# A four-layer graph network in one kernel: keys and queries from one projection, and the first node tile loaded in parts

## The chip, the cores and the metric

The kernel runs on one core of one Trainium2 chip. The metric is device time in microseconds (us) of one execution; lower is better. All executions quoted here were in the fast state, except one single run (named below) whose state is not known, and every kernel gave correct outputs.

## The reference, cut to what matters

There are 3327 nodes with 256 features. Four layers run one after the other, each as `x = layernorm(x + layer(x, adj))`. Layer 1 (graph convolution and a state-space scan) is not touched. The parts that the change touches:

```python
# layer 0
deg = adj.sum(axis=1, keepdims=True) + 1.0
neigh = adj @ features / deg
out0 = jnp.concatenate([features, neigh], axis=-1) @ W.T

# layer 2: attention on the graph; its normalised output is layer 3's X

# layer 3: two steps, each with a fresh attention over all nodes
for n in range(2):
    q = Xa @ W1.T @ W2.T             # 64 columns
    k = Xa @ W3.T                    # 64 columns
    A = top_p(softmax(q @ k.T))      # keeps the largest 90% of each row's mass
    Xf = R @ Xf                      # R: row-normalised adjacency with ones added
    Xa = A @ Xa
    Z = Z + Xf @ U1[n].T + Xa @ U2[n].T
```

## The kernel before

Nodes are cut into 26 tiles of 128. TensorE does nearly all of the arithmetic in float32. A record is one line of the trace; one float32 matmul with a 128-row operand appears there as two, so "four records" below are two instructions.

Layer 0 loads all features at once, then works tile by tile. `aggregate` streams one tile's adjacency column blocks and sums 26 products (the 257th column is ones and gives the degree):

```python
def aggregate(atp, psum, it, rhs, cols, jh=JH):          # JH = 13 blocks a load
    acc = psum.tile([P, cols], F32, name="acc")
    for j0 in range(0, nt, jh):
        m = min(jh, nt - j0)
        at = atp.tile([P, jh, P], F32, name="at")
        nc.sync.dma_start(at[:, :m, :], a["adjT"][it][:, j0:j0 + m, :])
        for j in range(m):
            nc.tensor.matmul(acc, at[:, j, :], rhs[:, j0 + j, :], ...)
    return acc
# ... layer 0:
xa = pool.tile([P, nt, D + 1], F32, name="xa")
nc.sync.dma_start(xa[:, :, :D], a["x"])                  # all features, 3.4 MB
nc.vector.memset(xa[:, :, D:], 1.0)
w0 = load(pool, "w0")
for it in range(nt):
    xt = work.tile([P, D // P, P], F32, name="xt")
    nc.sync.dma_start(xt, a["xT"][:, :, it * P:(it + 1) * P])
    acc = aggregate(atp, psum, it, xa, D + 1)
    # ... divide by the degree, transpose, product with w0, add, layernorm
```

Keys and queries are made tile by tile, at the end of layer 2 for step one and inside step one for step two. The 3328 padded nodes are two halves of 13 tiles. A key of the first half is kept on partitions 0 to 63, one of the second half on partitions 64 to 127, so that both halves use all partitions. A query is needed on both sets of partitions. In the kernel before, the weights are simply doubled (`wk` holds W3 twice, `wq` the query weights twice), and each tile pays two 128-column projections:

```python
def query(work, pq, xt):
    for k in range(2):
        nc.tensor.matmul(pq, wq[:, k, :], xt[:, k, :], start=(k == 0), stop=(k == 1))
    q = work.tile([2 * DA, P], F32, name="q")
    nc.scalar.copy(q, pq)
    return q

def key_and_query(work, ps, p, it, xt):
    for k in range(2):
        nc.tensor.matmul(ps[:, 0, :], wk[:, k, :], xt[:, k, :], start=(k == 0), stop=(k == 1))
    h, j = divmod(it * P, half)
    nc.scalar.copy(kT[p][h * DA:(h + 1) * DA, j:j + P], ps[h * DA:(h + 1) * DA, 0, :])
    nc.sync.dma_start(qd[p][it], query(work, ps[:, 1, :], xt))
```

Half of each key projection is thrown away. Layer 2 calls this one tile late, between two tiles' sums, so that the chain that normalises a tile has time to end:

```python
for it in range(nt):
    # ... VectorE builds the attention weights into "at" (two instructions for 13 blocks), 26 products into acc
    if it:
        project(it - 1)                    # transpose X of the tile before, then key_and_query
    # ... VectorE and ScalarE: divide, elu, add, statistics
    power(rs, mv)                          # GpSimd, two small instructions
    nc.gpsimd.tensor_scalar(X[:, it, :], o, mv[:, 0:1], rs, op0=ALU.subtract, op1=ALU.mult)
project(nt - 1)
```

## Time and profile before

| what | value |
|---|---|
| time, median of three runs (lowest, highest) | 4009.58 us (4000.31, 4012.51) |
| profiled run | 4007.87 us, span 4006.0 |
| matmul records on TensorE | 15071, busy 90% of the span |

The first lines of the page of the kernel before (busy us, share of the span, count of each engine):

```profile
span 4006.0 us, 41676 instructions
...
PE 3596.0 (90%) x15071; PEld 2625.0 (66%) x15071; DVE 2724.7 (68%) x6003; ACT 1675.1 (42%) x2690; POOL 367.1 (9%) x436
```

90% does not say where TensorE is free. The table of stretches of the same kernel does, here cut where the stages hand over to each other: at the last summing record of layer 0, the first of layer 2, the first of layer 3 and the last attention sum of step one (rows: layer 0; layer 1; layer 2; step one of layer 3; the rest. Columns: stretch, length, busy us and count of PE, PEld, DVE, ACT, POOL, granted clock, DMA share, GB/s):

```profile
0.00:362.00 362.00, 345.93 (x1602) 300.00 (x1603) 61.41 (x210) 22.04 (x55) 0.69 (x6) 1.00 0.46 153
362.00:1715.90 1353.90, 1125.40 (x3536) 654.14 (x3534) 1159.51 (x1145) 684.51 (x1230) 98.92 (x92) 0.92 0.11 36
1715.90:2068.80 352.90, 337.47 (x1612) 288.46 (x1613) 237.79 (x284) 43.50 (x130) 57.26 (x80) 0.96 0.37 125
2068.80:3034.40 965.60, 941.37 (x4503) 728.71 (x4504) 415.01 (x1410) 320.89 (x594) 28.39 (x56) 0.99 0.18 54
3034.40:4006.00 971.60, 845.79 (x3822) 653.70 (x3820) 850.96 (x2955) 604.14 (x681) 181.80 (x203) 0.94 0.19 54
```

The reader is to see that layer 0, layer 2 and step one leave TensorE idle for only 16, 15 and 24 us, and that the 16 us of layer 0 are the opening, before the first matmul.

### The profile page before, as it was taken

The page shows a single profiled execution, that of the slowest core. Times are in us where ns is not written, and L with a number is a line of the kernel's source. Part 1 is how long each engine was busy: PE and PEld are TensorE (multiplying, and loading weights), DVE is VectorE, ACT ScalarE, POOL GpSimd, SP SyncE. Part 2 cuts the span into 40 slices and gives each one's busy share as a digit, 9 for nine tenths or more (in the row PEclk, how much of TensorE's full clock was granted, in tenths as well). Part 3 has the DMA queues.
Part 4 walks back from the last instruction along what each step waited for, and adds up shares of the span by engine and source line. Part 5 has one row for each costly group of instructions (what it writes and reads, how often), then busy time and mean ns, then how long its engine had stood idle before and what let it go on. Part 6 is the DMA issues. An engine that isn't in the chain of part 4 may idle for free.

```text
span 4006.0 us, 41676 instructions
## 1 busy us (share of the span) xinstructions
PE 3596.0 (90%) x15071; PEld 2625.0 (66%) x15071; DVE 2724.7 (68%) x6003; ACT 1675.1 (42%) x2690; POOL 367.1 (9%) x436
## 2 busy tenths in 40 slices
PE   8999988888888877689999999999999899999985
PEld 7888754444444433378877777777777677777764
DVE  1111589999999989867743443443452999999996
ACT  0000555455554555211112333333344666666662
POOL 0000000101010101011110000000000122222210
PEclk9999999999999988889999999999999999999997
DMA  6442211111111000044422111121102122122100
GB/s 218 138 143 92 76 50 40 35 40 35 35 35 37 20 0 0 15 146 142 142 83 75 56 59 49 52 60 57 46 24 86 58 62 62 53 61 61 54 22 7
DMA packets 98960, 252.96 MB, mean 63 GB/s; under 512 B 13858, under 2 KB 48034, under 8 KB 98610
## 3 DMA queue, kind: packets, MB, share of 16 engines
q1 hardware_dynamic: 98738, 250.14, 20.0%
q8 instruction: 122, 2.00, 0.2%
q14 instruction: 100, 0.82, 0.1%
HBM read 239.88 MB, written 10.22 MB: 62 GB/s over the span
## 4 chain that ended last, share of the span: by engine, by line
PE 34%; DVE 16%; ACT 3%; issue 2%; POOL 2%; DMA 0%; POOLq 0%; ACTq 0%; DVEq 0%
PE acc L751 11%; PE acc L719 7%; PE acc L649 6%; PE sc L707 3%; DVE cand L759 3%; DVE e L892 2%; DVE e L893 2%; PE tp L747 2%; PE pj L917 1%; DVE z L829 1%; DVE top L768 1%; DVE z L873 1%; DVE rest L770 1%; ACT junk L827 1%; ACT junk L848 1%
## 5 line engine op out<-in xcount | busy, mean ns | idle before, releaser
L403 DVE TENSOR_TENSOR_SCAN h<-dA,carry,db 128x512 f32<-128x512 f32 (+1 forms) x448 | 510.7, 1191 | 0.1
L459 PE MATMUL y<-h,ident 128*128 128x512 f32 (+1 forms) x896 | 436.1, 633 | 76.7 <-DVE h L406 76.6
L759 DVE MAX8 cand<-e 128x8 f32<-128x128 f32 x676 | 143.8, 280 | 494.6 <-ACT e L708 494.6
L751 PE MATMUL acc<-G,wt 128*128 128x256 f32 x1352 | 342.9, 408 | 48.4 <-ACT wt L749 48.4
L459 PEld LDWEIGHTS y<-h,ident 128*128 128x128 f32 x896 | 185.9, 215 | 290.8 <-issue 175.9
L749 ACT COPY wt<-tp 128x512 f32<-128x512 f32 (+1 forms) x364 | 185.9, 552 | 438.3 <-PE tp L747 438.2
L751 PEld LDWEIGHTS acc<-G,wt 128*128 128x128 f32 x1352 | 268.9, 204 | 120.7 <-ACT wt L749 82.2
L234 PE MATMUL cb<-F,at 128*128 128x256 f32 x1352 | 334.2, 393 | 9.3 <-ACT m L251 9.2
L708 ACT COPY e<-sc 128x416 f32<-128x416 f32 (+1 forms) x416 | 192.5, 508 | 327.8 <-PE sc L707 327.8
L751 PE MATMUL acc<-X,wt 128*128 128x256 f32 x1352 | 326.0, 386 | 3.0 <-ACT wt L749 2.8
L719 PE MATMUL acc<-X,at 128*128 128x256 f32 x1352 | 320.8, 387 | 2.7 <-POOL e L701 2.7
L234 PEld LDWEIGHTS cb<-F,at 128*128 128x128 f32 x1352 | 261.1, 196 | 90.9 <-issue 33.5
L649 PE MATMUL acc<-F,at 128*128 128x257 f32 x1352 | 311.2, 384 | 2.5 <-DVE at L646 2.5
L719 PE MATMUL acc<-F,at 128*128 128x256 f32 x1352 | 308.8, 380 | 0.0
L113 PE MATMUL acc<-xa,at 128*128 128x257 f32 x1352 | 308.3, 381 | 0.0
L719 PEld LDWEIGHTS acc<-X,at 128*128 128x128 f32 x1352 | 250.8, 191 | 76.1 <-issue 41.8
L751 PEld LDWEIGHTS acc<-X,wt 128*128 128x128 f32 x1352 | 250.3, 191 | 63.8 <-ACT wt L749 33.5
L388 ACT ACTIVATE dA<-dt,A_log 128x512 f32<-128x512 f32 (+1 forms) x448 | 280.9, 681 | 12.6 <-DVE dt L365 12.2
L707 PE MATMUL sc<-kT,q 64*128 64x416 f32 x832 | 259.8, 561 | 26.0 <-ACT e L708 26.0
L113 PEld LDWEIGHTS acc<-xa,at 128*128 128x128 f32 x1352 | 255.7, 191 | 37.5 <-issue 0.7
L719 PEld LDWEIGHTS acc<-F,at 128*128 128x128 f32 x1352 | 249.5, 189 | 46.5 <-issue 13.7
L649 PEld LDWEIGHTS acc<-F,at 128*128 128x128 f32 x1352 | 254.1, 192 | 37.4 <-DVE at L646 2.7
(297 smaller groups left out, 5358.7 us busy)
## 6 DMA issues: line engine op xcount, KB each, us to landing
at<-in_adjT SPq DMA_DIRECT2D x104, 832.0 KB, 4.4
at<-in_adjT SPq DMA_DIRECT2D x156, 448.0 KB, 3.3
at<-in_adjT SPq DMA_DIRECT2D x52, 576.0 KB, 3.7
at<-in_adjT SPq DMA_DIRECT2D x52, 320.0 KB, 2.9
at<-in_adjT SPq DMA_DIRECT2D x26, 512.0 KB, 3.5
xa<-in_x SPq DMA_DIRECT2D x1, 3328.0 KB, 13.5
xt<-in_xT SPq DMA_DIRECT2D x26, 128.0 KB, 4.0
qd<-q SPq DMA_DIRECT2D x52, 64.0 KB, 1.5
```

Of the source, the lines that this page charges most:

```text
L113: nc.tensor.matmul(acc, at[:, j, :], rhs[:, j0 + j, :], start=(j0 + j == 0), stop=(j0 + j == nt - 1))
L234: nc.tensor.matmul(acc, at[:, j % JC, :], X0[:, j, :], start=(j == 0), stop=(j == nt - 1))
L388: nc.scalar.activation(dA[:, g, :], dt[:, g, :], AF.Exp, scale=A[:, g, s:s + 1])
L403: nc.vector.tensor_tensor_scan(h[:, g, :], dA[:, g, :], db[g // 2][:, g % 2, :], initial=carry[:, s, g:g + 1], op0=ALU.mult, op1=ALU.add)
L459: nc.tensor.matmul(ys[g][:, :w], ident, h[:, g, :], start=False, stop=(s == DS - 1))
L649: nc.tensor.matmul(acc, at[:, j, :], F[:, j0 + j, :], start=(j0 + j == 0), stop=(j0 + j == nt - 1))
L707: nc.tensor.matmul(pl[:, :w], q[h:h + DA, :], kT[p][h:h + DA, c0:c0 + w], start=True, stop=True)
L708: nc.scalar.copy(e[:, c:c + w], pl[:, :w])
L719: nc.tensor.matmul(acc, at[:, j, :], rhs[:, j0 + j, :], start=(j0 + j == 0), stop=(j0 + j == nt - 1))
L749: nc.scalar.copy(wt[:, :m, :], pt[:, :m, :])
L751: nc.tensor.matmul(acc, wt[:, j, :], rhs[:, j0 + j, :], start=(j0 + j == 0), stop=(j0 + j == nt - 1))
L759: nc.vector.max(cand[:, s * 8:(s + 1) * 8], z[:, s * SEG:(s + 1) * SEG])
```

## The change

Its intent is twofold. Both weight sets go into one 128-column operand, keys in one half and queries in the other, so one projection makes both. For the second half of the nodes the halves are swapped (`wkq[0]`, `wkq[1]`), so keys still land on the partitions where they are kept. The queries come out on one set of partitions only and are therefore written to memory twice. And the first tile of layer 0 is loaded in parts of four blocks, features and adjacency together, so that TensorE starts before all features have come.

```diff
-    def aggregate(atp, psum, it, rhs, cols, jh=JH):
+    def aggregate(atp, psum, it, rhs, cols, jh=JH, source=None):
...
+            if source is not None:
+                nc.sync.dma_start(rhs[:, j0:j0 + m, :D], source[:, j0:j0 + m, :])
             at = atp.tile([P, jh, P], F32, name="at")
...
-            nc.sync.dma_start(xa[:, :, :D], a["x"])
             nc.vector.memset(xa[:, :, D:], 1.0)
-            w0 = load(pool, "w0")
             for it in range(nt):
+                if it:
+                    acc = aggregate(atp, psum, it, xa, D + 1)
+                else:
+                    acc = aggregate(atp, psum, it, xa, D + 1, J0, a["x"])      # J0 = 4
+                    w0 = load(pool, "w0")
                 xt = work.tile([P, D // P, P], F32, name="xt")
                 nc.sync.dma_start(xt, a["xT"][:, :, it * P:(it + 1) * P])
-                acc = aggregate(atp, psum, it, xa, D + 1)
...
-        wk = pool.tile([P, 2, 2 * DA], F32, name="wk")
-        wq = pool.tile([P, 2, 2 * DA], F32, name="wq")
+        wkq = [pool.tile([P, 2, 2 * DA], F32, name=f"wkq{h}") for h in range(2)]
...
-                nc.scalar.copy(wq[:, k, :], pw)
+                for h in range(2):
+                    nc.scalar.copy(wkq[h][:, k, (1 - h) * DA:(2 - h) * DA], pw)
...
         def key_and_query(work, ps, p, it, xt):
+            h, j = divmod(it * P, half)
             for k in range(2):
-                nc.tensor.matmul(ps[:, 0, :], wk[:, k, :], xt[:, k, :], start=(k == 0), stop=(k == 1))
-            h, j = divmod(it * P, half)
-            nc.scalar.copy(kT[p][h * DA:(h + 1) * DA, j:j + P], ps[h * DA:(h + 1) * DA, 0, :])
-            nc.sync.dma_start(qd[p][it], query(work, ps[:, 1, :], xt))
+                nc.tensor.matmul(ps, wkq[h][:, k, :], xt[:, k, :], start=(k == 0), stop=(k == 1))
+            key, query = (slice(x * DA, (x + 1) * DA) for x in (h, 1 - h))
+            nc.scalar.copy(kT[p][key, j:j + P], ps[key, :])
+            q = work.tile([2 * DA, P], F32, name="q")
+            nc.scalar.copy(q[query, :], ps[query, :])
+            for x in (0, DA):
+                nc.sync.dma_start(qd[p][it, x:x + DA, :], q[query, :])
```

Cut from it: the callers' smaller PSUM tiles, and a rarely taken branch of layer 3 that did not run in any trace here.

More of the change, by code (lines that the diff above doesn't have):

```diff
@@ L22 @@
 JH = 13
+J0 = 4
 JC = 9
@@ L484, in gnn_kernel @@
         qd = [dram.tile([nt, 2 * DA, P], F32, name=f"qd{p}") for p in range(2)]
-        wk = pool.tile([P, 2, 2 * DA], F32, name="wk")
-        wq = pool.tile([P, 2, 2 * DA], F32, name="wq")
+        wkq = [pool.tile([P, 2, 2 * DA], F32, name=f"wkq{h}") for h in range(2)]
         with tc.tile_pool(name="l3a", bufs=1) as wpool, tc.tile_pool(name="l3ap", bufs=2, space=PSUM) as psum:
             w1 = load(wpool, "W1")
-            w2 = wpool.tile([DA, 2 * DA], F32, name="w2")
-            for h in (0, DA):
-                nc.sync.dma_start(w2[:, h:h + DA], a["W2"])
-                nc.sync.dma_start(wk[:, :, h:h + DA], a["W3"])
+            w2 = load(wpool, "W2")
+            for h in range(2):
+                nc.sync.dma_start(wkq[h][:, :, h * DA:(h + 1) * DA], a["W3"])
             for k in range(2):
@@ L498, in gnn_kernel @@
                 nc.scalar.copy(wt, pt)
-                pw = psum.tile([P, 2 * DA], F32, name="ps")
+                pw = psum.tile([P, DA], F32, name="ps")
                 nc.tensor.matmul(pw, wt, w2, start=True, stop=True)
-                nc.scalar.copy(wq[:, k, :], pw)
+                for h in range(2):
+                    nc.scalar.copy(wkq[h][:, k, (1 - h) * DA:(2 - h) * DA], pw)
         mhalf = pool.tile([P, 1], F32, name="mhalf")
@@ L508, in power, with key_and_query @@
             nc.gpsimd.tensor_tensor(rs, rs, mhalf, op=ALU.pow)
-        def query(work, pq, xt):
+        def key_and_query(work, ps, p, it, xt):
+            h, j = divmod(it * P, half)
             for k in range(2):
-                nc.tensor.matmul(pq, wq[:, k, :], xt[:, k, :], start=(k == 0), stop=(k == 1))
+                nc.tensor.matmul(ps, wkq[h][:, k, :], xt[:, k, :], start=(k == 0), stop=(k == 1))
+            key, query = (slice(x * DA, (x + 1) * DA) for x in (h, 1 - h))
+            nc.scalar.copy(kT[p][key, j:j + P], ps[key, :])
             q = work.tile([2 * DA, P], F32, name="q")
-            nc.scalar.copy(q, pq)
-            return q
-        def key_and_query(work, ps, p, it, xt):
-            for k in range(2):
-                nc.tensor.matmul(ps[:, 0, :], wk[:, k, :], xt[:, k, :], start=(k == 0), stop=(k == 1))
-            h, j = divmod(it * P, half)
-            nc.scalar.copy(kT[p][h * DA:(h + 1) * DA, j:j + P], ps[h * DA:(h + 1) * DA, 0, :])
-            nc.sync.dma_start(qd[p][it], query(work, ps[:, 1, :], xt))
+            nc.scalar.copy(q[query, :], ps[query, :])
+            for x in (0, DA):
+                nc.sync.dma_start(qd[p][it, x:x + DA, :], q[query, :])
         def layer2_any():
@@ L584, in layer2_any @@
                     xt = transposed(work, psum, X[:, it, :], "xt")
-                    key_and_query(work, psum.tile([P, 2, P], F32, name="ps"), 0, it, xt)
+                    key_and_query(work, psum.tile([P, P], F32, name="ps"), 0, it, xt)
         with tc.tile_pool(name="l2c", bufs=1) as cpool:
@@ L633, in project @@
                         xt = transposed(work, psum, X[:, it, :], "xt")
-                        key_and_query(work, psum.tile([P, 2, P], F32, name="ps"), 0, it, xt)
+                        key_and_query(work, psum.tile([P, P], F32, name="ps"), 0, it, xt)
                     for it in range(nt):
@@ L927, in first @@
             nc.scalar.copy(G[:, it, :], pg[:, 0, :])
-            key_and_query(work, pg[:, 1, :].rearrange("p (a b) -> p a b", a=2), 1, it, xt[:, 2:, :])
+            key_and_query(work, pg[:, 1, :P], 1, it, xt[:, 2:, :])
             yield
@@ L1079, in again @@
                     nc.vector.memset(pw[:, k:k + 1], 2.0 ** -(k + 1))
-                if p == 0:
-                    pt = psum.tile([P, 4, P], F32, name="pj")
-                    for k in range(2):
-                        nc.tensor.transpose(pt[:, k, :], X[:, it, k * P:(k + 1) * P], ident)
-                    xt = work.tile([P, 4, P], F32, name="xt", bufs=1)
-                    nc.scalar.copy(xt[:, :2, :], pt[:, :2, :])
-                    q = query(work, pt[:, 2, :], xt)
-                else:
-                    q = work.tile([2 * DA, P], F32, name="q")
-                    nc.sync.dma_start(q, qd[p][it])
+                q = work.tile([2 * DA, P], F32, name="q")
+                nc.sync.dma_start(q, qd[p][it])
                 e = work.tile([P, npad], F32, name="e", bufs=1)
```

## The prediction

> **What bounds the kernel now.** I read the page first, for the engine shares; then the table of stretches, cut at the first and last instruction of each layer, because a share over 4006 us mixes stages with different limits; then the timeline at the three places the change touches; last the waits of TensorE in the two steady stretches.
>
> The table of stretches (columns: stretch, length, busy us and count of PE, PEld, DVE, ACT, POOL, granted clock, DMA share, GB/s):
>
> ```profile
> 0.00:16.00 16.00, 0.00 (x0) 0.00 (x0) 0.87 (x9) 1.28 (x1) 0.69 (x6) 1.00 0.90 303
> 16.00:340.00 324.00, 323.93 (x1499) 280.86 (x1500) 57.33 (x190) 19.80 (x51) 0.00 (x0) 1.00 0.47 156
> 340.00:1705.00 1365.00, 1142.23 (x3608) 668.67 (x3607) 1157.44 (x1138) 680.46 (x1219) 98.92 (x92) 0.93 0.11 33
> 1705.00:2069.00 364.00, 342.83 (x1642) 293.28 (x1643) 243.07 (x303) 48.52 (x144) 57.46 (x80) 0.96 0.38 129
> 2069.00:3046.00 977.00, 952.78 (x4560) 737.75 (x4560) 416.55 (x1415) 322.63 (x599) 29.65 (x58) 0.99 0.19 55
> 3046.00:4006.00 960.00, 834.19 (x3765) 644.45 (x3764) 849.42 (x2950) 602.39 (x676) 180.35 (x201) 0.94 0.18 54
> ```
>
> Rows one to six are: the opening load with no matmul at all, layer 0, layer 1, layer 2, the first step of layer 3, its second step. TensorE is without a gap in layer 0 (323.93 of 324) and nearly so in layer 2 and the first step of layer 3 (97.5%). Layer 1 and the second step are shared between TensorE and VectorE, and the change does not touch them. So I expect a TensorE instruction saved in layer 2 or in step one to be time saved, and an earlier start to carry through layer 0.
>
> The timeline of one tile of layer 2 (columns: start, us, engine, line, operation):
>
> ```profile
> 1879.66 0.61 PE L520 MATMUL ps<-xt,wk 128*128 128x128 f32 x4
> ...
> 1880.11 0.60 PE L649 MATMUL acc<-F,at 128*128 128x257 f32 x2
> 1880.31 0.26 ACT L522 COPY kT<-ps 64x128 f32<-64x128 f32 x1 [0.89 <-PE ps L520]
> ...
> 1880.62 0.71 PE L512 MATMUL ps<-xt,wq 128*128 128x128 f32 x4
> ...
> 1881.17 1.03 PE L649 MATMUL acc<-F,at 128*128 128x257 f32 x4
> ...
> 1881.41 0.27 ACT L514 COPY q<-ps 128x128 f32<-128x128 f32 x1 [0.84 <-PE ps L512]
> ```
>
> Keys (L520) and queries (L512) are two projections of the same tile. The second begins only after the copy of the keys (L522) has ended at 1880.57: TensorE is held for it for the last few hundredths of a us. The same pair in the first step of layer 3:
>
> ```profile
> 2586.48 0.71 PE L520 MATMUL pj<-xt,wk 128*128 128x128 f32 x4
> ...
> 2587.02 0.60 PE L751 MATMUL acc<-X,wt 128*128 128x256 f32 x2
> ...
> 2587.54 0.71 PE L512 MATMUL pj<-xt,wq 128*128 128x128 f32 x4
> ...
> 2588.08 0.81 PE L751 MATMUL acc<-X,wt 128*128 128x256 f32 x3
> ```
>
> The opening, from the timeline of the first 60 us:
>
> ```profile
> 0.72 0.68 SPq L140 DMA_DIRECT2D xa<-in_x  x1
> ...
> 16.07 2.05 PE L155 MATMUL po<-w,xt 128*128 128x256 f32 x4 [16.07 <-DMA xt<-in_xT]
> ...
> 18.12 15.03 PE L113 MATMUL acc<-xa,at 128*128 128x257 f32 x58
> ...
> 31.88 0.16 DVE L148 TENSOR_SCALAR deg<-acc 128x1 f32<-128x1 f32 x1 [30.02 <-PE acc L113]
> ...
> 44.07 1.03 PE L155 MATMUL po<-w,xt 128*128 128x256 f32 x4
> ```
>
> Nothing is multiplied until all features (3.4 MB), the weights and xt have landed. Tile 0 is then summed by 31.88 and tile 1 by 44.07. The 58 records take 259 ns each, against 220 ns later, because the first ones run slow (six records between 18 and 20 us).
>
> **What the Trainium skill says.**
> - "TensorE: Matmul & The Clock Gate", Part 1: the array starts at half rate and goes to full rate after about 3.4 us of sustained work, and falls back after an idle window of that length. The trace agrees: about 430 ns a record until about 21 us, five us after the first matmul, then 220 ns. An earlier start pays this too, so I count it.
> - "PSUM — Partial Sum Buffer", the section on bank collisions: guard PSUM by bank and quadrant, because two engines must not touch the same one at once. Both projections write one tile, so the second has to wait for the reader of the first; the trace has that wait, 53 times and 17.9 us in all, summed over weight loads and matmuls.
> - "DMA: Bandwidth & Descriptors", Specifications: a fabric ceiling of 435 GB/s. The trace has 350 to 417 GB/s between 4 and 22 us, so cutting one load into parts cannot speed the stream, only let work start before its end.
>
> **The change part by part.**
>
> *One projection instead of two.* The key weights and the query weights become two halves of one 128-column operand; for the second half of the nodes the halves are swapped, so that the keys come out on the partitions where they are kept. Per tile, two matmuls (four records) go. Keys and queries are still two copies on ScalarE (64x128 each, near 0.26 us), and the write of the queries becomes two half writes.
>
> In layer 2: from the first key record to the first record after the queries is 1881.17 - 1879.66 = 1.51 us. Of this the four key records are 0.45 (to 1880.11) and the two summing records 2 x 0.22 = 0.44. What is left, 0.62 us, is the second projection with its wait (four records of about 0.11, an exposed weight load, 0.07 us of waiting). The stretch 1750 to 2045 has 291.6 of 295 us of TensorE busy, so all of it is on the path: 24 tiles x 0.62 = 14.9 us, rounded to 15. At the end of the layer the last tile is projected alone and slowly: the key copy ends at 2064.84, the query copy at 2066.47; the new pair of copies would end near 2065.1, so 1.4 us less, of which I give 0.3 back for the second half write.
>
> In the first step of layer 3: 2588.08 - 2586.48 = 1.60 us, less 0.54 for keys and 0.44 for summing, again 0.62 us. TensorE's waits in this stretch are only 22.7 us in 935, and VectorE is busy 43%, so the path is TensorE's: 26 x 0.62 = 16 us.
>
> *First tile in parts.* Features and adjacency arrive in seven parts of four blocks (512 + 256 KB), the weights and xt after them. My estimate, from bytes over the measured rates: the first bytes come at about 2.7 us, part one is complete at about 5.1, then one part each 2.2 us, the last near 16.5, weights and xt near 18, tile 1's two halves near 20.3 and 22.4. TensorE begins at about 5.1, slow for five us: part one ends at 8.7, the others follow at 0.22 us a record, always behind their data, and tile 0 is summed at about 19 instead of 31.88. The static order now puts tile 1 after tile 0's whole tail (sum, scale, transpose, copy, product), where before it overlapped: about 3 us in which TensorE mostly waits. Tile 1 then runs 52 records x 0.22 = 11.5 us, from 22.2 to 33.7 instead of 44.07. Gain: about 10.4 us, not the 11 us by which the first matmul is earlier. From there layer 0 has the same order and no gap, so it is carried to the end.
>
> *Small things.* The query weights are copied four times instead of twice before layer 2, at about 0.26 us each: 0.4 us lost.
>
> Sum: 15 + 1.1 + 16 + 10.4 - 0.4 = 42 us. The three runs of before average 4007.5, the profiled one took 4007.9; I subtract from about 4009: **3967 us**, 1.1% less.
>
> **The rivals.**
> - *The projection is hidden.* If step one were paced by the search on VectorE, its 16 us would not appear. Against: VectorE is busy 417 of 977 us, and its longest wait there is for scores that TensorE makes. It would make 3983.
> - *Layer 2 is paced by loads.* VectorE waits some 2.2 us a tile for adjacency. But those loads wait for buffers that TensorE frees, and the DMA share is 0.39. It would leave 3982.
> - *The opening is bound by the stream.* Tile 0 needs 5.1 MB, 14 us at 370 GB/s, and weights and tile 1 come behind it. If parts land later, or TensorE drops to the slow clock between parts or in the 3 us tail, the opening gains 5 rather than 10: 3972. If tile 1 starts at once, it gains 13: 3964.
> - *The second write delays the queue.* 52 more issues at about 0.33 us on the sync queue, 17 us in all, spread over 1341 us; adjacency loads behind them have buffers in hand. I give it 0 to 3 us.
>
> **Range and chances.** Both halves of the projection saving are read from gapless TensorE stretches; I give 25 to 34 us for them. The opening gets 5 to 13. The sum of the ends is 30 to 47; the runs of before spread over 12 us, so I widen to 27 to 54 below 4009: 3955 to 3982. Over 2% needs 80 us, which the change does not hold even if all went twice as well: 0.02. Slower by 2% would need a broken stage: 0.01. Within 2%: 0.97.
>
> **What the profile after would show.** Right: first matmul near 5 us; tile 0's sum near 19, tile 1's near 34; layer 0 ending 10 us earlier; 104 fewer records each in layer 2 and in step one; per tile of layer 2 about 0.6 us less and of step one 36.3 (36.9 before, from the transposes of xf at 2579.77 and 2616.67); layer 1 and the second step as long as before within the clock's variation. Wrong: the same tile period with a longer wait of TensorE for ScalarE's copies or for loads; a first tile still summed after 25 us; or a layer 1, untouched, that changes by more than 10 us through the granted clock (0.93 there), which would shift the total without this change's doing.

## The result, and the profile after

| | before | after |
|---|---|---|
| median of four runs | 4011.05 us | 3964.2 us |
| lowest, highest | 4000.31, 4019.0 | 3958.67, 3973.81 |
| ratio after : before, 95% interval | | 0.9887, 0.9857 to 0.9918 |

A ratio is the mean time of one kernel's fast runs over that of the other's of the same rounds, so it is not quite the ratio of the medians. The change is a gain of 1.1%, within the 2% that counts as the same. The same kernel, run again later on another chip beside the kernel before, gave a ratio of 0.9908 (0.989 to 0.9925): the size of the gain is 37 to 45 us.

The page of the kernel after, first lines:

```profile
span 3960.8 us, 41368 instructions
...
PE 3568.0 (90%) x14863; PEld 2605.8 (66%) x14863; DVE 2724.9 (69%) x6003; ACT 1677.1 (42%) x2692; POOL 367.0 (9%) x436
```

208 records fewer on TensorE: 52 tiles of four. The table of stretches of the kernel after, cut at the same events and with the columns as before:

```profile
0.00:352.00 352.00, 345.41 (x1602) 299.52 (x1603) 61.39 (x210) 22.05 (x55) 0.69 (x6) 1.00 0.48 158
352.00:1705.12 1353.12, 1134.03 (x3536) 658.38 (x3534) 1158.98 (x1145) 685.20 (x1232) 98.88 (x92) 0.92 0.12 36
1705.12:2038.10 332.98, 316.77 (x1508) 274.02 (x1509) 238.49 (x284) 44.76 (x130) 57.14 (x78) 0.98 0.41 132
2038.10:2989.10 951.00, 925.21 (x4404) 719.78 (x4405) 415.00 (x1410) 320.95 (x594) 28.52 (x57) 0.99 0.19 55
2989.10:3960.80 971.70, 846.55 (x3818) 654.14 (x3816) 851.05 (x2955) 604.13 (x681) 181.80 (x203) 0.94 0.19 54
```

Layer 0 is 10.0 us shorter, layer 2 is 19.9, step one is 14.6, and the two untouched stretches stayed as they were (-0.8 and +0.1). Layer 2 gave more than the 16 us predicted for it, and that is one of the things to explain.

One tile of layer 2 in the timeline of the kernel after (start, us, engine, line, operation):

```profile
1906.37 0.38 PE L101 MATMUL ps<-ident,X 128*128 128x128 f32 x2
...
1907.46 0.61 PE L519 MATMUL ps<-xt,wkq 128*128 128x128 f32 x4
...
1907.90 10.60 PE L651 MATMUL acc<-F,at 128*128 128x257 f32 x48
...
1908.10 0.26 ACT L521 COPY kT<-ps 64x128 f32<-64x128 f32 x1 [0.89 <-PE ps L519]
1908.39 0.26 ACT L523 COPY q<-ps 64x128 f32<-64x128 f32 x1
1908.67 1.09 SPq L525 DMA_DIRECT2D qd<-q  x2
```

The summing records (L651) follow the one projection at once and run on for 48 records. The two copies on ScalarE now lie beside them and hold nobody. A step-one tile, same view:

```profile
2541.55 0.38 PE L913 MATMUL pj<-ident,xf 128*128 128x128 f32 x2
...
2548.26 0.70 PE L519 MATMUL pj<-xt,wkq 128*128 128x128 f32 x4
...
2577.82 0.38 PE L913 MATMUL pj<-ident,xf 128*128 128x128 f32 x2
```

From transposes to transposes it is 36.27 us, against 36.90 in the pair of rows that the prediction names. The opening of the kernel after:

```profile
5.93 13.93 PE L116 MATMUL acc<-xa,at 128*128 128x257 f32 x52 [5.93 <-DMA at<-in_adjT]
19.70 0.59 PE L160 MATMUL po<-w,xt 128*128 128x256 f32 x2
20.92 0.41 PE L101 MATMUL ps<-ident,m 128*128 128x128 f32 x2 [0.63 <-DVE m L156]
...
22.76 11.47 PE L116 MATMUL acc<-xa,at 128*128 128x257 f32 x52
34.06 1.03 PE L160 MATMUL po<-w,xt 128*128 128x256 f32 x4
```

Tile 0 is summed by 19.70 us, tile 1 by 34.06. TensorE waits only 0.63 us in the tail between them, but does little more there than tile 0's own small products.

### The profile page after: what moved, and what is told of

Its sections match the earlier page's. It is cut to its first block, busy times and chain, and to the rows that moved or that the text cites. A ratio compares the mean times of both kernels' runs of the same rounds, so it can differ in the third digit from the quotient of the medians.

```text
span 3960.8 us, 41368 instructions
## 1 busy us (share of the span) xinstructions
PE 3568.0 (90%) x14863; PEld 2605.8 (66%) x14863; DVE 2724.9 (69%) x6003; ACT 1677.1 (42%) x2692; POOL 367.0 (9%) x436
## 4 chain that ended last, share of the span: by engine, by line
PE 34%; DVE 16%; ACT 3%; issue 2%; POOL 2%; DMA 0%; POOLq 0%; ACTq 0%; DVEq 0%
PE acc L753 12%; PE acc L721 8%; PE acc L651 6%; PE sc L709 3%; DVE cand L761 3%; DVE e L894 2%; DVE e L895 2%; PE tp L749 2%; PE pj L919 1%; DVE top L770 1%; DVE z L831 1%; DVE z L875 1%; ACT junk L829 1%; DVE rest L772 1%; POOL rs L513 1%
## 5 line engine op out<-in xcount | busy, mean ns | idle before, releaser
L464 PE MATMUL y<-h,ident 128*128 128x512 f32 (+1 forms) x896 | 445.3, 644 | 72.6 <-DVE h L411 72.4
L651 PE MATMUL acc<-F,at 128*128 128x257 f32 x1352 | 303.9, 381 | 1.1 <-DVE at L648 1.1
L393 ACT ACTIVATE dA<-dt,A_log 128x512 f32<-128x512 f32 (+1 forms) x448 | 281.0, 681 | 12.6 <-DVE dt L370 12.2
L651 PEld LDWEIGHTS acc<-F,at 128*128 128x128 f32 x1352 | 253.7, 191 | 36.8 <-DVE at L648 1.4
```

Of the source, the lines that this page charges most:

```text
L393: nc.scalar.activation(dA[:, g, :], dt[:, g, :], AF.Exp, scale=A[:, g, s:s + 1])
L464: nc.tensor.matmul(ys[g][:, :w], ident, h[:, g, :], start=False, stop=(s == DS - 1))
L651: nc.tensor.matmul(acc, at[:, j, :], F[:, j0 + j, :], start=(j0 + j == 0), stop=(j0 + j == nt - 1))
```

## The experiments

**The theories.** The prediction's theory: in the steady tiles TensorE is the path, so a tile is worth its four records plus the wait and the exposed weight load between the two projections; and the opening gains about what tile 1 ends earlier. Its rivals: the projection is hidden behind something else (nothing would come back if records were added); the opening is set by the data stream and not by TensorE's slow clock; layer 2's surplus is chance, or it is a real effect of a shorter tile.

Layer 1, which no kernel here touches, took between 1348 and 1363 us over the twelve profiles of the experiments. That is more than any single term, so terms are judged by stage lengths and by tiles, and totals only by ratios over several rounds. The stage lengths of all profiles, in us, cut at the same events as above:

| kernel | layer 0 | layer 1 | layer 2 | step one | rest |
|---|---|---|---|---|---|
| before | 362.0 | 1353.9 | 352.9 | 965.6 | 971.6 |
| before_again | 360.5 | 1357.2 | 349.3 | 965.3 | 970.6 |
| after | 352.0 | 1353.1 | 333.0 | 951.0 | 971.7 |
| after_again | 352.0 | 1357.8 | 336.5 | 951.3 | 973.7 |
| e1_projection | 360.9 | 1350.5 | 340.3 | 950.7 | 971.5 |
| e2_parts | 352.1 | 1357.6 | 351.6 | 964.5 | 972.1 |
| e4_no_wait | 360.9 | 1363.4 | 346.2 | 961.2 | 966.3 |
| e5_twice | 351.9 | 1352.3 | 343.9 | 964.1 | 969.6 |
| e6_j13 | 355.2 | 1348.3 | 332.1 | 951.0 | 971.8 |
| e7_j2 | 357.7 | 1359.8 | 344.7 | 952.8 | 973.5 |
| e10_warm | 352.0 | 1358.0 | 334.6 | 949.9 | 969.4 |
| e9_late | 351.6 | 1361.9 | 322.6 | 949.7 | 968.2 |
| late_again | 351.9 | 1356.1 | 323.9 | 950.6 | 968.8 |
| e11_before_late | 361.8 | 1351.7 | 340.2 | 964.9 | 970.0 |

### The projection alone

```diff
 # the kernel after, with the opening of the kernel before
+nc.sync.dma_start(xa[:, :, :D], a["x"])
+w0 = load(pool, "w0")
 for it in range(nt):
+    # xt loaded ahead of the tile; no parts
     acc = aggregate(atp, psum, it, xa, D + 1)
```

> Only the joint projection; features, weights and first tile loaded as before. Theory: the two parts are independent and add, so this keeps the savings of layer 2 and of layer 3's first step: first matmul at 16.1 us again, layer 0's last tile at 348.9 as before, one tile of layer 3's first step 36.27 us (36.90 before), total 32 to 35 us under before (about 3977). Rival (the saving in layer 2 and step one is partly a shifted start of those stages, or chance of the granted clock): under 25 us. If the extra 3 us of layer 2 come from the slow clock being met once less at its start and not from the change, layer 2 may save 15 here and not 18.

Measured: median 3975.27 us against 4010.75 of the same rounds, ratio 0.9919 (0.989 to 0.9948), so some 32 us. Layer 0 stayed at 360.9, step one fell to 950.7, layer 2 to 340.3. The projection is the larger part of the gain. Layer 2 fell by less than in the kernel after; the section on layer 2 below says why.

### The parts alone

```diff
 # the kernel before, with the opening of the kernel after
+J0 = 4
+            acc = aggregate(atp, psum, it, xa, D + 1, J0, a["x"])     # for tile 0
```

> Only the loading in parts; two projections as before. Theory: first matmul at 5.9 us, tile 0 summed at 19.6, tile 1 at 33.9, layer 0's last tile at 338.9 (348.9 before), every later stage as long as before, total 10 us under before (about 4000). Rival (an earlier layer 0 is taken back by the loads of layer 1's weights, which then come closer to their use): layer 1 begins 10 us earlier but is longer, total within 4 us of before.

Measured: median 3997.63, ratio 0.9967 (0.9958 to 0.9977), 13 us by the ratio. Layer 0 took 352.1, and layer 2 and step one are those of the kernel before (351.6, 964.5). So the earlier start is carried through layer 0 to the end. The two parts alone sum to 0.81% + 0.33% = 1.14%; together they gave 1.13% and, in the second run, 0.92%. They add, as far as this can be told.

### Two projections without the wait between them

```diff
 # the kernel before; both projections are issued before any copy reads their PSUM tile
 for k in range(2):
     nc.tensor.matmul(ps[:, 0, :], wk[:, k, :], xt[:, k, :], start=(k == 0), stop=(k == 1))
+for k in range(2):
+    nc.tensor.matmul(ps[:, 1, :], wq[:, k, :], xt[:, k, :], start=(k == 0), stop=(k == 1))
 nc.scalar.copy(kT[p][...], ps[..., 0, :])
+nc.scalar.copy(q, ps[:, 1, :])
```

> The kernel before with both projections issued before either copy, so that the query matmuls no longer wait for the key copy; same instructions, same count. Theory (the work is what costs, 0.45 us of the 0.62 are the four records): saves the exposed weight load and the 0.07 us of waiting, 0.17 us a tile, 50 tiles, 6 to 9 us in all; a tile of layer 3's first step 36.7 us. Rival (the wait for the key copy is what costs): 20 us or more, a tile of step one near 36.35 us.

Measured: median 3996.04, ratio 0.9968 (0.9956 to 0.9979). The timeline of one tile of layer 2 in this kernel:

```profile
1910.32 0.38 PE L100 MATMUL ps<-ident,X 128*128 128x128 f32 x2
1910.54 1.03 PE L653 MATMUL acc<-F,at 128*128 128x257 f32 x4
1911.41 0.61 PE L520 MATMUL ps<-xt,wk 128*128 128x128 f32 x4
1911.85 0.61 PE L522 MATMUL ps<-xt,wq 128*128 128x128 f32 x4
...
1922.74 0.38 PE L100 MATMUL ps<-ident,X 128*128 128x128 f32 x2
```

The query projection starts 0.44 us after the key projection, back to back. The tile is 1922.74 - 1910.32 = 12.42 us, against 12.59 before: 0.17 us saved. A tile of step one is 36.71 us (2579.19 to 2615.90), against 36.90. So the wait and the exposed weight load are worth 0.17 to 0.19 us a tile, and layer 2 and step one are shorter by 5 and 4 us than the means before, the 6 to 9 us expected. The total fell by more, 13 us by the ratio; in the profile the rest took 966.3, 4 to 5 us less than before, which was not explained. Some 9 us of the change could be had by ordering alone.

### The joint projection done twice

```diff
-            for k in range(2):
-                nc.tensor.matmul(ps, wkq[h][:, k, :], xt[:, k, :], start=(k == 0), stop=(k == 1))
+            for _ in range(2):
+                for k in range(2):
+                    nc.tensor.matmul(ps, wkq[h][:, k, :], xt[:, k, :], start=(k == 0), stop=(k == 1))
```

> The changed kernel with the joint projection done twice over into the same place (same result): four records a tile come back, no wait and no copy with them. Theory: each record costs 0.11 us of TensorE and nothing hides it, so 0.44 us a tile more than the changed kernel, 52 tiles, 22 to 24 us; a tile of step one 36.7 us. Rival (TensorE has slack and the gain came from the wait and from the copies): under 8 us.

Measured: median 3981.56, ratio 0.9929 (0.9905 to 0.9953). The timeline of layer 2:

```profile
1923.30 0.38 PE L101 MATMUL ps<-ident,X 128*128 128x128 f32 x2
...
1924.39 1.05 PE L520 MATMUL ps<-xt,wkq 128*128 128x128 f32 x8
...
1935.72 0.38 PE L101 MATMUL ps<-ident,X 128*128 128x128 f32 x2
```

Again 12.42 us, which is 0.45 more than the 11.97 of the joint projection done once; step-one tiles again take 36.72 (2559.94 to 2596.66), 0.45 more. Four records added come back as four records of time in the steady tiles of both stages. The rival that something hides the projection falls. The stages give back less than the 22 to 24 us expected: 20.0 (343.9 and 964.1 against means of 336.9 and 951.1 with the projection done once), and by the ratios it is 8 or 17 us, depending on which run of the kernel after is taken. The shortfall is in layer 2, 7.0 us: in this profile the second wait at the start of the layer, described below, happened not to come. With the experiment before it the 0.62 us of a tile is divided: 0.45 for four records, 0.17 for the wait and the exposed load.

### The parts made larger, and smaller

```diff
-J0 = 4
+J0 = 13        # e6_j13: two parts of 1664 + 832 KB
```

> The changed kernel with parts of 13 blocks instead of four. Theory (the opening is TensorE's from its first matmul on, half of it on the slow clock, so the start decides; the order of this variant overlaps tile 0's tail with tile 1): first part of 2.5 MB complete near 9.9 us, tile 0 summed near 23.9, tile 1 near 37, so 3 us more than the changed kernel (tile 1 at 33.9) and 7 less than before (44.1). Rival (the stream bounds the opening): tile 0 near 20 and tile 1 as in the changed kernel.

```diff
-J0 = 4
+J0 = 2         # e7_j2: thirteen parts of 256 + 128 KB
```

> The changed kernel with parts of two blocks. Theory: first matmul near 4.7 us, slow until about 9.7, then 0.88 us of TensorE a part against 1.07 us of stream, so TensorE catches up with the data: tile 0 near 18, tile 1 near 32.5, one us less than the changed kernel. Rival (the sync queue, 26 issues of about 0.5 us, and four buffers bound it): tile 0 later than 20 us.

Measured: 3964.71 (0.9891, 0.9871 to 0.9912) with parts of 13, and 3975.55 (0.9908, 0.9885 to 0.9932) with parts of 2. The totals of the parts of 13 and of 4 are not to be told apart; the openings are. With parts of 13:

```profile
10.33 13.89 PE L116 MATMUL acc<-xa,at 128*128 128x257 f32 x52 [10.33 <-DMA at<-in_adjT]
24.07 1.02 PE L160 MATMUL po<-w,xt 128*128 128x256 f32 x4
```

The first part takes 10.33 us to come, and tile 0 is summed by 24.07; layer 0 takes 355.2, 3.2 us more than with parts of 4, as expected. Tile 1 then overlaps tile 0's tail, which gives some of the late start back. With parts of 2:

```profile
4.11 2.05 PE L116 MATMUL acc<-xa,at 128*128 128x257 f32 x4 [4.11 <-DMA at<-in_adjT]
...
22.70 1.11 PE L116 MATMUL acc<-xa,at 128*128 128x257 f32 x4 [0.72 <-DMA at<-in_adjT]
```

TensorE starts earliest of all, at 4.11, but is kept waiting four more times (3.1 us), and tile 0 is summed near 23.8 (22.70 + 1.11), hardly earlier than with parts of 13; the rival was right. The stream itself has become slower: between 8 and 20 us it moves 269 GB/s on average, where parts of 4 have 375. Four adjacency buffers of two blocks hold little in flight, and the sync queue waits 6.1 us for TensorE to free them; that this is what slows the stream is argued, since no run here had more buffers. Layer 0 takes 357.7, 5.7 us more. Four blocks is a good choice between the two.

### A warm TensorE ahead of the first part

```diff
             xa = pool.tile([P, nt, D + 1], F32, name="xa")
+            full = work.tile([P, P], F32, name="full", bufs=1)
+            nc.vector.memset(full, 1.0)
+            warm = psum.tile([P, P], F32, name="warm", bufs=1)
+            for _ in range(10):
+                nc.tensor.matmul(warm, full, full, start=True, stop=True)
```

> The changed kernel with ten matmuls of a constant tile into a spare tile ahead of the first part (nothing reads it), to have TensorE on its full clock when data come. Theory (about eleven records of the opening run at 0.43 instead of 0.22 us): first real matmul still near 5.9, records of 0.22 us soon after, TensorE then waits for the stream, tile 0 summed near 17.5 instead of 19.6, tile 1 near 32, 2 us under the changed kernel. Rival (the slow start is not a matter of earlier work): the records after 5.9 stay at 0.43 us for another five us, no gain.

Measured: 3972.06, ratio 0.9911 (0.989 to 0.9932). The timeline of its opening:

```profile
5.67 4.63 PE L116 MATMUL acc<-xa,at 128*128 128x257 f32 x16
10.46 1.98 PE L116 MATMUL acc<-xa,at 128*128 128x257 f32 x8 [0.16 <-DMA at<-in_adjT]
12.65 1.98 PE L116 MATMUL acc<-xa,at 128*128 128x257 f32 x8 [0.21 <-DMA at<-in_adjT]
...
19.78 0.67 PE L165 MATMUL po<-w,xt 128*128 128x256 f32 x2
```

The warming took away most of the slow records: up to 9.6 us the table of stretches counts 15 records here (from 5.67) and 9 in the kernel after (from 5.93). Then TensorE waits for every part, one each 2.18 us, the sixth of seven at 17.01; 12 records of 0.22 us remain, 2.6 us. Tile 0 is summed at 19.78, where the kernel after had it at 19.70, and tile 1 at 34.06 in both (its row stands in the opening above). The 2 us expected did not come: without the slow start the stream ends tile 0 at the same time. In the kernel after no record waits for a part once the first has come, but TensorE reaches the sixth part at 17.09, about when it lands. So the slow clock of the first microseconds is hidden, and the two limits, TensorE's work and the stream, meet there.

### Layer 2: the projection one tile later

The kernel after's layer 2 gained 19.9 us in its first profile, 3.8 more than predicted for it. Both kernels lose time at the layer's start. In the kernel before:

```profile
1747.54 0.69 PE L100 MATMUL ps<-ident,X 128*128 128x128 f32 x2 [3.79 <-POOL X L668]
...
1764.20 0.69 PE L100 MATMUL ps<-ident,X 128*128 128x128 f32 x2 [3.07 <-POOL X L668]
1764.68 1.92 PE L649 MATMUL acc<-F,at 128*128 128x257 f32 x4
```

and in the kernel after:

```profile
1736.34 0.69 PE L101 MATMUL ps<-ident,X 128*128 128x128 f32 x2 [4.87 <-POOL X L670]
...
1752.26 0.44 PE L101 MATMUL ps<-ident,X 128*128 128x128 f32 x2 [2.61 <-POOL X L670]
1752.54 1.03 PE L651 MATMUL acc<-F,at 128*128 128x257 f32 x4
```

The bracket names GpSimd's last instruction of the normalisation: TensorE stands until the tile's features are there. After the second wait four summing records took 1.92 us (slow clock) in one kernel and 1.03 (full clock) in the other. That difference, some 4 us by the third tile (61.9 us after the first summing record before, 57.0 after, of which 1.2 are the change's), did not come from the change: the tile after the second wait took 10.7 to 13.6 us in the three profiles with two projections and this order, and 9.9 to 12.7 in the six with one, so both outcomes come in both. To remove the waits, projections were moved one tile later:

```diff
-                        if it:
-                            project(it - 1)
+                        if it > 1:
+                            project(it - 2)
...
+                    project(nt - 2)
                     project(nt - 1)
```

on the kernel after (`e9_late`, and again as `late_again`) and on the kernel before (`e11_before_late`).

> The changed kernel with each tile of layer 2 projected one tile later, so that its normalised features are long ready. Theory (layer 2 starts with two waits of TensorE for the normalised features, 7.5 us in the profile of the changed kernel, each followed by up to five us on the slow clock, and short ones later, now that the tile is shorter): those waits go, layer 2 takes 333 - 8 = 325 us, less 1 to 2 given back at its end where one more tile is left to project; 6 to 10 us under the changed kernel, near 3956. Rival (the first tiles are bound by VectorE's making of the weights, so the wait moves to the sum): within 2 us of the changed kernel.

Measured: 3956.16, ratio 0.9861 (0.9838 to 0.9884). Its layer 2 begins so:

```profile
1713.52 35.69 PE L651 MATMUL acc<-F,at 128*128 128x257 f32 x156 [3.47 <-DVE at L648]
1749.04 0.38 PE L101 MATMUL ps<-ident,X 128*128 128x128 f32 x2
...
1761.01 0.38 PE L101 MATMUL ps<-ident,X 128*128 128x128 f32 x2
```

156 summing records, three tiles, without a gap, and from there 11.97 us a tile. Layer 2 took 322.6 us, 10.4 less than the kernel after's first profile. Because the gain was less than a per cent and chips differ, the four kernels were then run on one chip:

> The changed kernel unaltered, for a second profile and a tighter time. Theory: ratio 0.988 to 0.990; layer 0, the steady tiles of layer 2 (11.97 us) and of layer 3's first step (36.27 us) as in its first profile within 0.1 us, while layer 1 and the first two tiles of layer 2 differ by several us between profiles of one kernel, so that layer 2's 19.9 us of saving in the first profile was 15 to 16 of the change and the rest chance. Rival: layer 2 again takes 333 us within one, so the extra is the change's.

> The kernel before unaltered, one more profile. Theory: layer 0 ends within 2 us of 362, steady tiles of 12.59 and 36.90 us again; layer 1 and the start of layer 2 differ by several us from the first profile.

> The changed kernel with the projection of layer 2 one tile later, once more beside the changed kernel on one chip. Theory: 6 to 10 us under the changed kernel of the same call. Rival (its gain was the chance of one sample): within 3 us of it.

> The kernel before with the projections of layer 2 one tile later, and nothing else. Theory (the waits at the start of layer 2 were there before the change, 6.9 us in its profile, with slow-clock tiles after them): 6 to 10 us under before. Rival (the waits matter only since the tile got shorter): under 3 us.

| same chip | median, us | ratio to before (95%) | layer 2, us |
|---|---|---|---|
| before_again (one run, state unknown) | 4004.78 | | 349.3 |
| after_again | 3971.83 | 0.9908 (0.989 to 0.9925) | 336.5 |
| late_again | 3954.41 | 0.9865 (0.9849 to 0.9882) | 323.9 |
| e11_before_late | 3998.38 | 0.9975 (0.9964 to 0.9985) | 340.2 |

The later projection is worth 12.6 us of layer 2 on the kernel after (336.5 - 323.9) and about 9 to 13 on the kernel before. The intervals of after_again and late_again do not meet: this version is faster than both kernels, by 54 us at the time before (1.35% of 4010). With it the joint projection saves 340.2 - 323.9 = 16.3 us of layer 2, which is the prediction's 16 (15 + 1.1) without the chance at the start (17.6 with the 322.6 of e9_late). Between after_again and late_again the totals differ by 17 us, more than the 6 to 10 expected; 5 us of it are in the rest (973.7 and 968.8), which this edit does not touch.

**What else scatters layer 2.** TensorE's waits for GpSimd's features in layer 2, its last tile included, from the same view of waits in each profile, beside the layer's length:

| kernel | waits, number | waits, us | layer 2, us |
|---|---|---|---|
| before, before_again, e2_parts | 3 each | 10.6, 12.2, 11.6 | 352.9, 349.3, 351.6 |
| after, e6_j13, e10_warm | 3 each | 12.4, 12.8, 11.2 | 333.0, 332.1, 334.6 |
| after_again, e1_projection | 5 each | 14.0, 16.2 | 336.5, 340.3 |
| e7_j2 | 4 | 18.8 | 344.7 |
| e4_no_wait (two projections, 12.42 us a tile) | 3 | 10.8 | 346.2 |
| e5_twice (joint projection, 12.42 us a tile) | 4 | 11.4 | 343.9 |
| e9_late, late_again, e11_before_late | 1 each | 2.9, 2.9, 1.9 | 322.6, 323.9, 340.2 |

Three of the six profiles with the joint projection done once have additional waits in the middle of the layer, and so has e5_twice (1.86 and 1.87 us); none of the four with two projections and the early order has. The longest is in the trace of e7_j2, in order of time:

```profile
1802.87 1.89 DVE L648 SCALAR_TENSOR_TENSOR at<-at,w 128x1664 f32<-128x1664 f32 x1
1802.96 1.89 POOL L512 TENSOR_SCALAR rs<-mv 128x1 f32<-128x1 f32 x1 [11.77 <-DVE mv L85]
...
1804.80 1.89 DVE L645 TENSOR_TENSOR w<-r,q 128x1664 f32<-128x1664 f32 x1
1804.94 2.18 POOL L513 TENSOR_TENSOR rs<-rs,mhalf 128x1 f32<-128x1 f32 x1
...
1808.51 0.69 PE L101 MATMUL ps<-ident,X 128*128 128x128 f32 x2 [4.84 <-POOL X L670]
```

GpSimd's instruction on 128x1 elements, 0.23 us in other tiles, took 1.89: it began 0.09 us after a long VectorE instruction and ended with it. The next, 0.57 elsewhere, began 0.14 us after the next VectorE instruction, and took 2.18. So TensorE waited 4.84 us for a tile and fell to the slow clock. In after_again and e1_projection it is the last GpSimd instruction that took 2.94 to 2.95 us instead of 1.23.

The waits at the start of the layer are in part the same thing. In all fourteen profiles the first two tiles have such slow GpSimd instructions: in the kernel before 1.85 us instead of 0.23 at 1742.44 and 1760.30, and 2.43 instead of 1.23 at 1745.06, each begun while a long VectorE instruction ran. With the projection one tile later they are still there (4.40 us at 1738.71 in late_again, and 2.94 at 1803.85 in mid-layer), but TensorE no longer waits for them.

"SBUF — State Buffer" of the Trainium skill, section "Who interferes with whom", states that a VectorE instruction with two SBUF inputs contends with a GpSimd instruction that reads SBUF, and that the later one is blocked; both VectorE instructions of the extract have two SBUF inputs, and the times agree for GpSimd. The shorter tile does bring the two engines' instructions closer together: from the start of GpSimd's last instruction to the next long VectorE instruction it is 1.2 to 1.3 us (median over the middle tiles of a profile) with two projections, 1.0 to 1.1 in e4_no_wait and e5_twice, and 0.6 with the joint projection. That this is why the mid-layer waits come is argued, not tested: of the two kernels with tiles of 12.42 us one has them and one has not, and no experiment here moved the normalisation off GpSimd.

## Why the prediction was right

Predicted were 3967 us and a range of 3955 to 3982. The first runs gave 3964.2, the later ones 3971.8, both inside.

- **What bounds the kernel.** Right. In layer 2 and step one, records added to TensorE lengthened the steady tiles by their own time (e5_twice), and layer 0's earlier start reached the end (e2_parts). The 97.5% that the prediction reads for both stages is step one's; layer 2's row gives 94.2% (342.83 of 364), with its waits at both ends.
- **A tile's 0.62 us.** Right in both stages and in its parts: 12.59 to 11.97 and 36.90 to 36.27. The four records measured 0.45, the rest 0.17 (e4_no_wait).
- **Layer 2, 15 + 1.1 us.** Right in size where nothing else moves: 16.3 between the two kernels with the late projection. As the change stands the term varied: 19.9 in the first pair of profiles, and 14.4 between the means (351.3 of the three profiles with two projections, 336.9 of the six with one done once and early). What the prediction left out is the layer's waits for GpSimd: those at its start, whose following clock is chance, and those in mid-layer, which no early-order profile with two projections shows.
- **Step one, 16 us.** Mis-sized by 2: the means are 965.1 (before, before_again, e2_parts) and 951.1 (after and the five other profiles of the joint projection), so 14.0. A steady tile saves what was predicted; the multiplication by all 26 tiles is what failed. The last tile's projection begins 6.5 us after the stage's last sum (3040.88 against 3034.41), outside the stage, and up to the second tile's transposes of xf nothing is saved (means of 141.0 and 141.5 us). From there to the end the means are 824.1 and 809.7, some 14.5 us for the 24 tiles between.
- **The opening, 10.4 us.** About right in size: 10.0 at layer 0's end in the first pair, and 361.2 less 352.0 = 9.2 between the means. Tile 1 was summed at 34.06 where 33.7 was said, tile 0 at 19.90 (VectorE's first reading of it, the mark that 31.88 is) where 19 was said. "Always behind their data" held, with nothing to spare: the first part was 0.8 us later (5.93, not 5.1), the parts then came every 2.2 us as said, and TensorE reached the sixth at 17.09, which the warmed kernel shows landing at 17.01. (The last part "near 16.5" was a slip in the sum: 5.1 + 5 x 2.2 + 1.1 is 17.2.) So the stream would end tile 0 no earlier, which the prediction did not see. The rival that the stream bounds the opening was half right about the cause and wrong about the loss: it would have left 5 us of gain, and 9 to 10 are there. The kernel before's own slow start was read too short: its records stay slow until 22.53 us, not 21. That stretch differs by chance, 6.5 us there and 3.4 in before_again, and layer 0 took 362.0 and 360.5 us accordingly; with parts of 4 it took 351.6 to 352.1 in all seven profiles.
- **The second write.** 52 more issues cost nothing that shows. They take longer than said: a median of 0.48 us each, against 0.32 for the single write, so the sync queue is busy some 34 us more and not 17. In the steady tiles nothing waits for them; at the end of layer 2 GpSimd waits for the last write, 6.1 us, as it did before (6.6). The 0.4 us of setup is under what these runs can tell.
- **The sum.** By stage means 14.4 + 14.0 + 9.2 = 37.6 us, against 42 predicted and 37 to 45 by the two ratios. That the first run came within 3 us of 3967 is in part luck: layer 2's start was a fast one.

## What to carry to other kernels

When one operand is half wasted, fill the half with the other projection: the gain is the records plus the wait between two users of one PSUM tile, and it can be read beforehand from one steady tile of a stage where TensorE has no gap. A gain of one per cent is judged by tiles and stages, since an untouched stage alone can move by 15 us between runs. And a tile that gets shorter leaves less time for the chain behind it: look at what is handed over one tile later and whether two tiles later is free, which here gave another 12.6 us.

## What the Trainium skill lacked or had wrong

- "TensorE: Matmul & The Clock Gate", Part 1, ties the fall to the slow clock to an idle window of about 3.4 us. It says that the window runs freely, but its rule of thumb names only gaps longer than that. Here, at the start of layer 2, a gap of 2.52 us was followed by slow records (e10_warm, four summing records in 1.92 us), one of 2.61 by fast ones (1.03), and one of 3.07 by slow ones. The gap alone does not tell, and gaps clearly under 3.4 us can cost.
- The same page and part: about 3.4 us of sustained work until the full clock, and a change seen at 4 us, give or take 0.5, because the window runs freely. The spread here is wider. With TensorE at work throughout, the first record of 0.22 us came 4.8 us after the first matmul in the kernel after (5.93 to 10.78), 6.5 in the kernel before (16.07 to 22.53) and 3.4 in before_again (16.11 to 19.52). In e10_warm it came 6.0 us after the first warming matmul (1.07 to 7.07). The table of stretches gives a granted clock of 1.00 in these slices, so that column does not show this slow state.
- "SBUF — State Buffer", section "Who interferes with whom", agrees for a GpSimd instruction that starts second (1.85 to 1.89 us instead of 0.23). The page's "Summary: rules for kernel authors" says of this pair that the second one to issue "fully blocks", and that was not seen the other way round: in late_again the VectorE instruction with two SBUF inputs that began 0.41 us into GpSimd's 1.23 took 1.89 us, as ever, and one that began 0.19 us into it in the kernel after took 2.10. Where VectorE's began only 0.01 to 0.11 us after GpSimd's, it was GpSimd's, the first to start, that took 2.94 to 2.95 us instead of 1.23 (after_again, e1_projection, late_again, e5_twice). Spans on GpSimd are rough in this profile.
- "DMA: Bandwidth & Descriptors", section "Bandwidth", asks for 1 MiB and more a transfer. It lacks the case of several smaller ones in flight: transfers of 512 and 256 KB in turn moved 375 GB/s here (8 to 20 us of the kernel after), and the loss only came with 256 and 128 KB and four buffers (269 in e7_j2).
